# A new table of turns for a cross-attention kernel in f32: every operation numbered anew, with the arithmetic left as it was

## The chip, the cores and the metric

The kernel runs on one core of one Trainium2 chip. The metric is the device time of one execution in microseconds (us); smaller is better. A kernel's time is the median of its runs.

## What is computed

The reference, cut to what matters (B = 2 sequences of S = 2048 tokens, H = 640, 8 heads of 80, a context of 124 text tokens and 4 adapter tokens of 384 numbers each, all f32):

```python
query = x @ Wq
hs = mha(query, enc @ Wk, enc @ Wv)            # text attention, 124 keys
ca_q1 = einsum('btc,th->bch', ca, Wq_ca)[:, linspace(0, 383, 2048).astype(int), :]
ca_hs1 = mha(ca_q1, x, x)                      # attention over all 2048 tokens, 384 distinct queries
ca_hs2 = mha(ca_hs1 @ Wq, ca @ Wk_ca, ca @ Wv_ca)   # 4 keys
out = (hs + ca_hs2) @ Wout + b_out + x
```

## The kernel before, in words

The work is cut into 8 blocks of 512 tokens, (b, sb), and 16 units of 256 tokens, each two tiles of 128. The names below are those of the tiles, as rows of the profile show them; a number behind a name is a block, a unit or a part.

**The first block's rows.** `first_loads` (line 667) loads x's first 512 rows on SyncE as four transfers into `xz`, and Wq on ScalarE's queue as chunks into `wq_sb`. `idle_work` (line 768) gives TensorE 14 products of zeros (`unread<-zeros`) to run while there is nothing else. `x_first` (line 828) transposes the first block on TensorE (`pt_x`): two of its five column chunks from `xz` itself, three from `first_rows`, which VectorE gathers by five small copies for each tile. The results are copied to `xt` by VectorE or ScalarE.

**Later blocks.** `x_load` (line 1347) fetches the rows on SyncE by 13 transfers into `xi`, eight of them of 1024 short pieces (32x32 rows of 32 numbers; the second of each pair is issued in line 1363). When all have landed, VectorE turns them by five stream transposes into `xt`. `load_wout` (line 1187) loads Wout on SyncE too: two transfers of 640 KB, eight small ones.

**Queries.** `queries` and `queries_fast` (lines 1400 and 1542) multiply `xt` by `wq_sb` (`pq`), the later ones by a scheme of Strassen's kind that needs sums of blocks, `x_sums` and `wq_sums`; the same is done for the output with `hs` and `wout_sums`.

**The adapter.** `yz_block` (line 1754) turns each block into `zop`, by products (`pyz`), moves and a two-input operation on VectorE (`zop<-zop,low_z,zb`). `adapter` (line 1869) has two stages. In the first, TensorE writes scores `s1` of 2048 columns into one set of four PSUM banks (the quad), and VectorE takes the largest of each (`mx<-s`, 2.3 us); 24 of them for each sequence. There is one quad, so the next `s1` has to wait for the `mx` of the one before. In the second stage ScalarE reads the quad instead (`ea<-s`, exponentials, 1.9 us) and TensorE contracts `ea` with the rows `y_sb` (`acc`).

**Text attention.** `text_scores` and `softmax` (lines 2140 and 2178): scores `sc`, a maximum `m` on VectorE, exponentials `p` on ScalarE, a reciprocal `r`, `p<-p,r` on GpSimd, VectorE or ScalarE, a transpose `eb` on VectorE; `eb` goes to HBM and comes back turned as `pT`.

**Outputs.** `text_out_fast` (line 2392): `ph` from `pT`, copies and sums in `hs`, products `po` with `wout_sb` and `wout_sums`, and VectorE adds them into `x_more` or `last_rows`, which hold the residual. GpSimd adds the adapter's rows by an indirect transfer (line 2351). `stored` and `stored_half` (lines 2508 and 2499) store the rows from SyncE's or ScalarE's queue; the last unit goes out in four halves.

**What sets the order.** Nothing above is issued in the order in which it is written. Each stage is a generator that yields operations (`Do`). `Desk.run` (line 351) takes, of all that wait, the one with the lowest number in the table `Desk.TURNS` (lines 85 to 291), and the number's remainder by 6 names the engine (PE, ACT, DVE, POOL, SP, or none). So the table sets the order of each engine's instructions and, where an operation may run on several engines, which one takes it: copies out of PSUM on VectorE or ScalarE, sums on VectorE or GpSimd, stores on SyncE or ScalarE. On the chip each engine runs its own list in order and waits for semaphores of the others. In the profile nearly all of it carries the line of a helper: 396, 405 and 410 for TensorE's products, products by columns and transposes, 427 for VectorE, ScalarE and GpSimd, 447 for transfers.

Of the kernel before, what the change touches and what calls it, by code (L numbers as in the profile page):

```python
# [65 lines left out]
class Desk:  # L66
# [19 lines left out]
        ".1": [995], ".2": [44, 59, 60, 84, 96, 108, 114, 120, 126, 132, 150, 174, 198, 210, 234, 978], ".3": [608],  # L86
        ".4": [5, 52, 76, 82, 94, 106, 352, 412, 442], ".4.1": [37, 67, 169, 241, 265], ".5": [468, 499, 534, 547,
        558, 584, 590], ".6": [11, 17, 144, 162, 204, 222, 258, 294, 300, 329], ".6.1": [140], ".6.2": [188],
        ".6.3": [218], ".6.4": [284], ".6.5": [157], ".6.6": [194], ".6.7": [229], ".6.8": [253], ".6.9": [278],
        ".6.10": [314], ".6.11": [319], ".7": [290, 510, 530, 1058], ".8": [23, 29, 35, 180, 246, 270, 306, 360,  # L90
        384, 396, 420, 426, 456, 486, 540, 576, 636, 726, 792, 803], ".8.1": [404], ".8.2": [416], ".8.3": [518],
        ".8.4": [703], ".8.5": [935, 1003, 1064, 1069, 1334], ".8.5.1": [1174], ".8.5.2": [1258], ".8.5.3": [1301],
        ".8.5.4": [1307, 1372, 1529, 1531, 1541, 1597], ".8.5.5": [1426], ".8.5.6": [1414], ".8.5.7": [1481],
        ".8.5.8": [1619, 1660, 1781, 1783, 1937, 1975], ".9": [368, 377, 450, 474, 485, 522, 564, 575, 618, 624,
        635, 672, 708, 762, 786], ".9.1": [464], ".9.2": [493], ".9.3": [553], ".9.4": [596], ".9.5": [643], ".9.6":
        [650], ".9.7": [685], ".9.8": [770], ".9.9": [812], ".9.10": [817], ".10": [605, 678, 716, 734, 828, 848,
        858, 919, 926, 936, 950, 972, 1088], ".11": [656, 744, 834, 912, 942, 960, 1025, 1031, 1039, 1052, 1084,
        1168, 1264, 1360, 1408, 1471], ".11.1": [782], ".11.2": [872], ".11.3": [956], ".11.4": [968], ".11.5":
        [1016], ".12": [1103, 1113, 1364], ".13": [760, 778, 1270], ".14": [724, 1176, 1214, 1308, 1328, 1416, 1441,
        1446, 1465, 1490, 1642, 1834, 1870, 1948, 2782, 4306, 5614, 6568], ".15": [694, 699, 984, 1032, 1242, 1272,  # L100
        1343], ".15.1": [1076], ".15.2": [1094], ".15.3": [1279], ".15.4": [1315], ".16": [1509], ".17": [335, 1104,
        1141, 1147, 1157, 1160, 1183, 1196, 1220, 1285, 1352], ".17.1": [1544, 1588, 1592, 1612, 1715, 1721, 2596,
        2830, 3832, 4780], ".18": [341, 1139], ".19": [809, 2663], ".20": [346, 358, 382, 394, 436, 448, 508, 616,
        664, 671, 752, 824, 842, 854, 866], ".21": [881, 1794, 1843, 1861, 1877, 1880, 1897, 1958, 1982, 2029,
        2078], ".21.1": [1886, 1912, 2084, 2116, 2219, 2225, 2362, 2734, 3028, 5020], ".22": [893, 2201], ".23":
        [2171, 3683], ".24": [887, 1128, 1200, 1320, 1344, 1392, 1458, 1482, 1644, 1704, 1740, 1836, 1926, 1950,
        2016, 2154, 2165], ".24.1": [1573], ".24.2": [1495], ".24.3": [1807], ".24.4": [1963], ".24.5": [2213, 2239,
# [2484 lines left out]
```

## Time and profile before

| | us |
|---|---|
| the three runs | 574.08, 573.70, 573.08; median 573.70 |
| the profiled execution | 573.39 |
| its span, first to last instruction | 571.3 |
| TensorE busy in the span | 563.5 (99%) |
| VectorE, ScalarE, GpSimd busy | 394.3, 287.0, 159.9 (69%, 50%, 28%) |
| TensorE's granted clock | 1.0 throughout |
| TensorE waited for another engine, all waits that the view lists | 3.5 |

The profiled execution took 573.39 us, 2.1 us more than its span, and lies 0.31 us below the median of the runs. Matmuls are pipelined and their ends are modelled, each about a quarter of a microsecond past the start of the next, so a wait of TensorE shows as idle time only in so far as it is longer than that. Starts are not modelled; a wait is best read from the start of the instruction that waited and the end of what it waited for.

### The profile page before, as it was taken

Reading aid. Unit: us, or ns where it says so; the run is one execution under the profiler, and the core shown is the slowest. Engines: PE = TensorE matmul, PEld = TensorE weight load, DVE = VectorE, ACT = ScalarE, POOL = GpSimd, SP = SyncE. Lnnn points to the kernel's source line nnn. Section 1 sums busy time; section 2 is a strip of 40 time slices with the busy share of each in tenths; the row PEclk is TensorE's granted clock in tenths of the full one; section 3 lists DMA queues with packets and bytes.
Section 4 is the critical chain, followed back from the end, with each engine's and each line's share of the span. In section 5 each row is a group of like instructions: output and inputs, shape, how many; then the busy total and the mean of one; then the engine's idle time right before and its main releaser. Section 6 shows DMA issues by size and latency. Waiting matters only on the chain.

```text
span 571.3 us, 18875 instructions
## 1 busy us (share of the span) xinstructions
PE 563.5 (99%) x8069; PEld 309.8 (54%) x8069; DVE 394.3 (69%) x659; ACT 287.0 (50%) x806; POOL 159.9 (28%) x213
## 2 busy tenths in 40 slices
PE   8999999999999999999999999999999999999997
PEld 8885335455555455466554554554555444455553
DVE  4366999999998577458999999998332213544443
ACT  2021355645566899899876654524554674100000
POOL 9102041114440731100004350531203053045152
PEclk9999999999999999999999999999999999999999
DMA  8998485965978877446746979987375587788887
GB/s 246 211 247 136 130 162 149 170 187 138 209 214 156 213 182 211 146 129 195 230 157 200 317 190 310 244 237 241 72 263 120 162 199 231 247 209 213 265 185 206
DMA packets 145691, 113.21 MB, mean 198 GB/s; under 512 B 82548, under 2 KB 116980, under 8 KB 145608
## 3 DMA queue, kind: packets, MB, share of 16 engines
q1 hardware_dynamic: 137144, 95.43, 59.8%
q0 software_dynamic: 5632, 10.69, 11.5%
q10 hardware_dynamic: 2832, 5.90, 3.0%
q8 instruction: 63, 1.03, 0.8%
q14 instruction: 20, 0.16, 0.1%
HBM read 71.60 MB, written 40.39 MB: 196 GB/s over the span
## 4 chain that ended last, share of the span: by engine, by line
PE 93%; ACT 3%; DVE 3%; DMA 1%; issue 0%; SPq 0%; ACTq 0%
PE po L405 27%; PE pq L405 24%; PE sc L396 8%; PE acc L396 7%; PE ph L396 7%; PE s L396 7%; PE pq L396 4%; PE pyz L396 2%; ACT ea L427 2%; PE pv L396 1%; DVE mx L427 1%; PE pk L396 1%; DMA xz<-in_x_dram 1%; ACT p L427 1%; PE pt_wq L410 1%; PE pw L396 0%
## 5 line engine op out<-in xcount | busy, mean ns | idle before, releaser
L427 ACT ACTIVATE p<-sc,m 128x124 f32<-128x124 f32 x256 | 90.4, 382 | 43.1 <-DVE m L427 38.1
L427 DVE TENSOR_REDUCE mx<-s 128x4 f32<-128x2048 f32 x48 | 108.9, 2270 | 1.9 <-PE s L396 1.9
L427 ACT ACTIVATE ea<-s 128x2048 f32<-128x2048 f32 x48 | 90.5, 1886 | 32.5 <-PE s L396 32.0
L405 PE MATMUL po<-wout_sums,hs 128*32 128x320 f32 x1024 | 78.4, 434 | 0.1
L405 PE MATMUL po<-wout_sb,hs 128*32 128x320 f32 x928 | 72.3, 433 | 0.0
L427 POOL TENSOR_TENSOR p<-p,r 128x992 f32<-128x992 f32 x17 | 31.4, 1849 | 130.9 <-DVE r L427 130.9
L405 PE MATMUL pq<-xt,wq_sb 128*32 128x256 f32 (+1 forms) x928 | 66.4, 418 | 0.0
L427 DVE TENSOR_TENSOR last_rows<-last_rows,po 128x320 f32<-128x320 f32 x60 | 28.1, 480 | 44.0 <-PE po L405 43.9
L427 ACT ACTIVATION_READ_ACCUMULATOR p<-sc,m 128x1 f32 x256 | 57.2, 224 | 0.0
L427 DVE TENSOR_TENSOR x_more<-x_more,po 128x320 f32<-128x320 f32 x68 | 32.3, 481 | 34.7 <-PE po L405 34.2
L405 PEld LDWEIGHTS po<-wout_sums,hs 128*32 128x32 f32 x1024 | 33.3, 110 | 32.7 <-issue 2.8
L427 DVE TENSOR_REDUCE m<-sc 128x4 f32<-128x496 f32 x64 | 40.7, 661 | 14.1 <-PE sc L396 14.0
L396 PE MATMUL acc<-ea,y_sb 128*32 128x384 f32 (+2 forms) x768 | 50.2, 382 | 0.2 <-ACT ea L427 0.2
L396 PE MATMUL ph<-pT,vpad 128*32 128x256 f32 x768 | 48.0, 381 | 0.1
L405 PEld LDWEIGHTS po<-wout_sb,hs 128*32 128x32 f32 x928 | 30.1, 110 | 28.3 <-issue 1.6
L2351 POOL DMA_INDIRECT x_more<-o,query x17 | 26.6, 1564 | 64.9 <-DVE x_more L427 30.7
L405 PEld LDWEIGHTS pq<-xt,wq_sb 128*32 128x32 f32 x928 | 27.7, 110 | 28.0 <-issue 13.4
L427 ACT COPY hs<-ph 128x512 f32<-128x512 f32 (+1 forms) x25 | 13.4, 552 | 57.7 <-PE ph L396 57.7
L427 DVE STREAM_TRANSPOSE eb<-p 128x1024 f32<-128x1024 f32 x32 | 39.4, 1230 | 1.2 <-POOL p L427 1.1
L396 PEld LDWEIGHTS sc<-kmain,q 64*128 64x128 f32 x512 | 31.8, 187 | 12.6 <-issue 5.8
L427 POOL TENSOR_TENSOR hs<-hs 128x256 f32<-128x256 f32 x31 | 28.9, 1021 | 34.2 <-ACT hs L427 26.0
L396 PE MATMUL sc<-kmain,q 64*128 64x124 f32 x512 | 38.0, 285 | 0.0
(219 smaller groups left out, 834.5 us busy)
## 6 DMA issues: line engine op xcount, KB each, us to landing
kept<-eb SPq DMA_DIRECT2D x32, 512.0 KB, 4.7
pT<-kept SPq DMA_DIRECT2D x16, 1024.0 KB, 7.8
landing<-away SPq DMA_DIRECT2D x15, 512.0 KB, 4.8
xi<-in_x_dram SPq DMA_DIRECT2D x56, 128.0 KB, 4.1
x_more<-in_x_dram SPq DMA_DIRECT2D x17, 320.0 KB, 4.8
last_rows<-in_x_dram SPq DMA_DIRECT2D x15, 320.0 KB, 6.3
y<-yt SPq DMA_DIRECT2D x16, 256.0 KB, 2.9
y_sb<-y SPq DMA_DIRECT2D x32, 128.0 KB, 3.9
```

The lines of the kernel that those rows point to most:

```text
L396: self.pin(self.nc.tensor.matmul(out, lhsT, rhs, **kw))
L405: self.pin(self.nc.tensor.matmul(out[j : j + 32], lhsT[:, j : j + 32], rhs, **kw))
L410: self.pin(self.nc.tensor.transpose(out, in_, ident))
L427: self.pin(getattr(engine, what)(*args, **kw))
L2351: desk.pin(nc.gpsimd.indirect_dma_start(out=t, out_offset=None, in_=o2_of[b], in_offset=bass.IndirectOffsetOnAxis(ap=query[:, st : st + 1] ...
```

## The change

The table of turns is replaced by another; no other line of the kernel differs. What it does, counted over the program: 3787 of TensorE's 4494 matmuls stand in the same order as before, nearly all of the others in the first 44 us and behind 306 us. Six sums move from GpSimd to VectorE, eight copies (net) from ScalarE to VectorE, and two stores from SyncE to ScalarE. The number of matmuls and their shapes are the same.

The table has 206 lines; of one of them, before and now:

```diff
-        ".1": [995], ".2": [44, 59, 60, 84, 96, 108, 114, 120, 126, 132, 150, 174, 198, 210, 234, 978], ".3": [608],
+        ".1": [875], ".2": [44, 59, 60, 78, 90, 102, 108, 114, 120, 138, 198, 204, 282, 354, 522, 858], ".3": [428],
```

The numbers tell a reader nothing, so here are the instructions at three places, before and now.

**The first microseconds.** ScalarE's first instructions before; the first DMA row stands for Wq's chunks 0 and 1, one behind the other, and the copies move transposed rows of the first block out of PSUM:

```order
L447 DMA wq_sb<-in_L_xattn_Wq_dram 128x640 x2
L427 ACT_TABLE_LOAD
L427 COPY xt_0_164<-pt_x_0_191 128x256
L447 DMA wq_sb<-in_L_xattn_Wq_dram 64x640 x2
L427 COPY xt_0_164<-pt_x_0_214 128x256
L447 DMA wq_sb<-in_L_xattn_Wq_dram 64x640 x2
L427 COPY xt_0_164<-pt_x_1_223 128x384
```

And now:

```order
L447 DMA wq_sb<-in_L_xattn_Wq_dram 128x640
L427 ACT_TABLE_LOAD
L427 COPY xt_0_164<-pt_x_0_184 128x256
L447 DMA wq_sb<-in_L_xattn_Wq_dram 128x640
L447 DMA wq_sb<-in_L_xattn_Wq_dram 64x640 x2
L427 COPY xt_0_164<-pt_x_1_199 128x384
L427 COPY xt_0_164<-pt_x_0_215 128x256
```

Wq's chunk 1 is issued behind the first copy instead of ahead of it. On GpSimd, at the end of its masks, before (`vpad` and `ca` are cleared, then `ca` is filled by small transfers):

```order
L541 AFFINE_SELECT band_c_148<-band_c_148 128x4
L427 MEMSET vpad_107 128x768
L427 MEMSET vpad_108 128x768
L427 MEMSET ca_152 128x384
L427 DMA ca_152<-in_ctx_dram 4x384 x16
```

And now:

```order
L541 AFFINE_SELECT band_c_148<-band_c_148 128x4
L427 MEMSET ca_152 128x384
L427 DMA ca_152<-in_ctx_dram 4x384 x16
L427 MEMSET vpad_107 128x768
L427 MEMSET vpad_108 128x768
```

The two clears of `vpad` stand behind `ca` and its 16 transfers now. On TensorE, 7 products of zeros instead of 8 stand ahead of the first transpose, and the eighth is done later among the first products.

**The third block's rows and the first maxima.** SyncE's queue before, from Wout's two large transfers on (`xi_2` is the block b = 0, sb = 2; `k_away` is a store of keys):

```order
L447 DMA wout_sb<-in_L_xattn_Wout_dram 64x4x640 x2
L447 DMA xi_2_521<-in_x_dram 32x32x32
L1363 DMA xi_2_521<-in_x_dram 32x32x32
L447 DMA xi_2_521<-in_x_dram 32x16x16 x2
L447 DMA xi_2_521<-in_x_dram 32x32x32
L1363 DMA xi_2_521<-in_x_dram 32x32x32
L447 DMA k_away<-k_parts 32x4x248
```

And now:

```order
L447 DMA xi_2_476<-in_x_dram 32x32x32
L1363 DMA xi_2_476<-in_x_dram 32x32x32
L447 DMA xi_2_476<-in_x_dram 32x16x16 x2
L447 DMA wout_sb<-in_L_xattn_Wout_dram 64x4x640
L447 DMA xi_2_476<-in_x_dram 32x32x32
L1363 DMA xi_2_476<-in_x_dram 32x32x32
L447 DMA wout_sb<-in_L_xattn_Wout_dram 64x4x640
L447 DMA k_away<-k_parts 32x4x248
```

Wout's two transfers of 640 KB stand between the block's pieces instead of ahead of them. VectorE, between the first two maxima of the adapter, before:

```order
L427 TENSOR_REDUCE mx_0_563<-s1_0_0_0_0_704 128x4
L427 STREAM_TRANSPOSE xt_0_2_703<-xi_0_2_521 128x512
L427 TENSOR_SCALAR blk_v_127<-pt_vca_734,side2_83 128x4x2x4 x2
L427 TENSOR_TENSOR blk_v_127<-pt_vca_734,eighth_87 128x4x8 x2
L427 TENSOR_TENSOR first_rests_532<-pq_0_2_168,first_rests_532 128x256
L427 SCALAR_TENSOR_TENSOR zop_0_0_666<-zop_0_0_666,low_z_134,zs_0_0_1_700 128x512
L427 TENSOR_REDUCE counted_162<-steps_597 128x16
L427 TENSOR_TENSOR counted_162<-counted_162,first_161 128x16
L427 CAST query_111<-counted_162 128x16
L427 STREAM_TRANSPOSE xt_0_2_703<-xi_0_2_521 128x512 x2
L427 TENSOR_REDUCE mx_0_563<-s1_0_0_0_1_768 128x4
```

And now:

```order
L427 TENSOR_REDUCE mx_0_663<-s1_0_0_0_0_704 128x4
L427 COPY vpad_0_107<-pv_0_1_577 124x4x64
L427 COPY vpad_0_107<-pv_0_1_577 124x2x16 x2
L427 SCALAR_TENSOR_TENSOR zop_0_0_667<-zop_0_0_667,low_z_134,zs_0_0_1_702 128x512
L427 TENSOR_SCALAR blk_v_127<-pt_vca_735,side2_83 128x4x2x4 x2
L427 TENSOR_TENSOR blk_v_127<-pt_vca_735,eighth_87 128x4x8 x2
L427 COPY vpad_1_108<-pv_1_1_727 124x4x64
L427 COPY vpad_1_108<-pv_1_1_727 124x2x16 x2
L427 STREAM_TRANSPOSE xt_0_2_700<-xi_0_2_476 128x512 x3
L427 COPY vpad_1_108<-pv_1_0_719 124x4x64
L427 COPY vpad_1_108<-pv_1_0_719 124x2x16 x2
L427 TENSOR_REDUCE mx_0_663<-s1_0_0_0_1_767 128x4
```

Nine copies into `vpad` have come to VectorE from ScalarE, the counting is done earlier, and the three transposes of the third block's rows stand together ahead of the second maximum.

**A maximum of the second sequence.** VectorE near 303 us of the trace, before (the names end in numbers of their own in each program):

```order
L427 TENSOR_REDUCE m_1_7_1_4053<-sc_1_7_1_4035 128x4
L427 SCALAR_TENSOR_TENSOR zop_1_1_3403<-zop_1_1_3403,low_z_134,zb_1_1_1_4014 128x512
L427 STREAM_TRANSPOSE eb_11_0_4107<-p_0_830 128x1024
L427 TENSOR_TENSOR q_7_3752<-q_7_3752,pq_7_3_3983 128x2x256
L427 TENSOR_REDUCE mx_1_3167<-s1_1_1_0_0_4115 128x4
L427 TENSOR_TENSOR x_sums_873<-pq_7_4_4017,x_sums_873 128x256
L427 TENSOR_TENSOR wout_sums_4129<-wout_sb_100 128x640
L427 TENSOR_TENSOR wq_sums_834<-pq_7_4_4017,wq_sums_834 128x256
L427 RECIPROCAL r_1_7_4054<-r_1_7_4054 128x8
L427 TENSOR_REDUCE mx_1_3167<-s1_1_1_0_1_4158 128x4
```

And now:

```order
L427 TENSOR_REDUCE m_1_7_1_4046<-sc_1_7_1_4028 128x4
L427 TENSOR_TENSOR q_7_3752<-q_7_3752,pq_7_3_3977 128x2x256
L427 STREAM_TRANSPOSE eb_11_0_4106<-p_0_830 128x1024
L427 SCALAR_TENSOR_TENSOR zop_1_1_3400<-zop_1_1_3400,low_z_134,zb_1_1_1_4006 128x512
L427 TENSOR_REDUCE mx_1_3071<-s1_1_1_0_0_4112 128x4
L427 TENSOR_TENSOR wout_sums_4129<-wout_sb_100 128x640
L427 TENSOR_TENSOR x_sums_871<-pq_7_4_4011,x_sums_871 128x256
L427 RECIPROCAL r_1_7_4047<-r_1_7_4047 128x8
L427 TENSOR_TENSOR wq_sums_834<-pq_7_4_4011,wq_sums_834 128x256
L427 TENSOR_REDUCE mx_1_3071<-s1_1_1_0_1_4156 128x4
```

`zop` goes behind `q` and `eb`, the last ahead of the maximum; GpSimd's list here is the same (`p<-p,r`, then `wout_sums<-wout_sb`).

**The last stores.** TensorE's last products are the same four groups for unit 15 as before. Before, SyncE issued the last half of unit 15 and behind it a store of a whole tile of unit 8 (`last_rows`); now ScalarE issues that tile of unit 8 (`x_more`) behind the third half, and SyncE's last instruction is the last half (`last_rows`).

410 rows, old and new, of the table TURNS are left out of this document.

## The prediction, made before the changed kernel was run

> **What bounds the kernel now.** I read the page first, its busy times, its slices and the chain:
>
> ```profile
> PE 563.5 (99%) x8069; PEld 309.8 (54%) x8069; DVE 394.3 (69%) x659; ACT 287.0 (50%) x806; POOL 159.9 (28%) x213
> ...
> DVE  4366999999998577458999999998332213544443
> ...
> PE 93%; ACT 3%; DVE 3%; DMA 1%; issue 0%; SPq 0%; ACTq 0%
> ```
>
> TensorE (PE) is busy for 563.5 us of 571.3 and carries 93% of the chain. VectorE (DVE), at 69% over the whole, is full in slices 5 to 12 and 20 to 27 of 14.3 us. So I asked for the windows of these stretches, and for TensorE's waits (the last row is one of them):
>
> ```profile
> core 0: us, PE busy (x) PEld busy (x) DVE busy (x) ACT busy (x) POOL busy (x), PEclk, DMA share, GB/s
> 0.00:57.00 57.00, 55.43 (x412) 44.24 (x413) 28.90 (x106) 10.13 (x21) 19.03 (x92) 1.00 0.92 210
> 57.00:171.00 114.00, 114.00 (x1562) 55.62 (x1565) 111.97 (x146) 60.53 (x228) 32.15 (x24) 1.00 0.71 170
> 171.00:271.00 100.00, 99.63 (x1631) 56.03 (x1625) 67.14 (x112) 87.87 (x228) 19.80 (x24) 1.00 0.68 176
> 271.00:385.00 114.00, 112.39 (x1657) 59.74 (x1655) 110.23 (x136) 68.93 (x268) 35.21 (x31) 1.00 0.79 236
> 385.00:571.30 186.30, 182.03 (x2824) 94.16 (x2822) 76.08 (x164) 59.50 (x63) 53.68 (x43) 1.00 0.74 201
> ...
> PE s L396 <- ACT ea L427: 0.6, 3, 0.2
> ```
>
> TensorE's idle time is 1.57 us in the first window, 0, 0.37 and 1.61 in the next three, and 4.27 in the last, nearly all of that behind its last product. The work of TensorE is not changed, so what a new order can gain is small: these waits, those too short to show, and the tail. What it can lose has no such bound, above all in the two stretches where VectorE has 2.0 and 3.8 us to spare in 114.
>
> **The change, part by part.** I take TensorE's list first. Its products are the same, but it changes between shapes of the array 263 times instead of 261. From 57 to 171 us it makes dozens of such changes with 0.00 us idle, so one costs less than the quarter of a microsecond by which ends are modelled; between 0 and 0.25 each I take 0.12: **+0.25**.
>
> *The start.*
>
> ```profile
> 1.13 3.59 PE L396 MATMUL unread<-zeros 128*128 128x128 f32 x16 [1.13 <-DVE zeros L427]
> 4.90 0.41 PE L410 MATMUL pt_x<-ident,xz 128*128 128x128 f32 x2 [0.18 <-POOL band_z L541]
> ...
> 7.90 0.52 PE L410 MATMUL pt_x<-ident,first_rows 128*128 128x128 f32 x3 [0.26 <-DVE first_rows L427]
> ...
> 9.80 1.89 PE L396 MATMUL pq<-xt,wq_sb 128*128 128x256 f32 x8
> 6.21 1.78 DVE L427 COPY first_rows<-xz 128x64 f32<-128x64 f32 x5 [0.75 <-DMA xz<-in_x_dram]
> 8.37 0.62 DVE L427 COPY first_rows<-xz 128x64 f32<-128x64 f32 x5
> 5.80 1.41 POOL L427 MEMSET vpad<- 128x768 f32 x2
> 5.35 1.17 ACTq L447 DMA_DIRECT2D wq_sb<-in_L_xattn_Wq_dram  x2
> DMA to landing us min/median/max: 3.2/4.0/4.9
> ```
>
> Five copies of first rows last 1.78 us beside GpSimd's (POOL's) clears of `vpad` and `ca`, and 0.62 without them; the transposes at 7.90 wait for them. The 0.26 of that row stands behind the modelled end of a pair of passes, about 0.4 long, of which 0.22 is issue (as at 4.90): 0.43 lost. With the clears of `vpad` moved behind the transfers of `ca` it goes. What is late next is x's second tile, which landed before 6.21 and lands no later now, since Wq's chunk 1 (320 KB) no longer stands beside it. A filler that stood under the first wait now stands among products: two passes of 0.11, +0.22. Against it the first transposes (4.90) may come up to 0.3 earlier with x's rows; I take 0.2. Chunk 1 is issued behind the first copy, as the row at 5.35 is now, and takes 3.2 to 4.9 us (the last row, of `wq_sb`'s transfers from 5 to 12 us), so it lands between 8.5 and 10.2; its first product stood at 9.80 and would stand at 9.4. The wait is 0 to 0.8, nearer 0.1 by the median of 4.0. Sum of the start: −0.43 + 0.22 − 0.2 + 0.1 = **−0.3** (−0.6 to +0.4).
>
> A rule speaks against it. The first 16 passes start 0.22 apart and later ones 0.11, at a granted clock that reads 1.0 throughout. The Trainium skill, "TensorE: Matmul & The Clock Gate", Part 1, says that the array runs at half speed until a window of about 3.4 us has been busy, and that the window runs free. By it, 14 passes that end at 4.3 could miss the window; that is rival D below.
>
> *The first maxima.*
>
> ```profile
> 40.88 4.85 SPq L447 DMA_DIRECT2D xi<-in_x_dram  x3
> 58.24 0.70 DVE L427 STREAM_TRANSPOSE xt<-xi 128x512 f32<-128x512 f32 x1
> 63.37 2.25 DVE L427 TENSOR_REDUCE mx<-s 128x4 f32<-128x2048 f32 x1
> 65.93 0.51 PE L396 MATMUL s<-zop,cop 32*128 32x512 f32 x4
> DMA to landing us min/median/max: 7.8/7.8/7.8
> ```
>
> The second maximum ends at 65.62, 0.31 ahead of the `s` that needs its quad. Between the two maxima VectorE now has nine `vpad` copies (0.2 us each in steps), `zop` and four `blk_v` (1.3), and three transposes (0.65 each in steps): about 5.2 us behind the maximum that ended near 58.3, so the next starts near 63.6 and ends at 65.9, and TensorE, whose list is 0.2 longer by there, waits 0 to 0.3: **+0.1**. Behind this stands SyncE: Wout's two transfers, 7.8 us from issue to landing (the last row), now lie between the block's pieces, in a queue that held a piece for 4.85 us. The pieces had landed when VectorE came at 58.24; it comes at about 61 now, so a delay of up to 2.8 us is covered. More is rival C.
>
> *The maximum at 307 us.*
>
> ```profile
> 303.53 2.00 DVE L427 SCALAR_TENSOR_TENSOR zop<-zop,low_z,zb 128x512 fp32r<-128x512 f32 x1
> 305.46 1.23 DVE L427 STREAM_TRANSPOSE eb<-p 128x1024 f32<-128x1024 f32 x1
> 306.62 0.64 DVE L427 TENSOR_TENSOR q<-q,pq 128x512 f32<-128x512 f32 x1
> 307.19 2.27 DVE L427 TENSOR_REDUCE mx<-s 128x4 f32<-128x2048 f32 x1
> 310.89 2.23 DVE L427 TENSOR_REDUCE mx<-s 128x4 f32<-128x2048 f32 x1
> 303.44 1.55 POOL L427 TENSOR_TENSOR wout_sums<-wout_sb 128x640 f32<-128x640 f32 x1 [0.64 <-PE pq L405]
> 305.84 0.51 PE L396 MATMUL s<-zop,cop 32*128 32x512 f32 x4
> 309.52 0.51 PE L396 MATMUL s<-zop,cop 32*128 32x512 f32 x4 [0.44 <-DVE mx L427]
> 313.17 0.51 PE L396 MATMUL s<-zop,cop 32*128 32x512 f32 x4 [0.67 <-DVE mx L427]
> L427 DVE SCALAR_TENSOR_TENSOR zop<-zop,low_z,zb 128x512 fp32r<-128x512 f32 x1 | 0.7, 741 | 0.0
> ```
>
> `zop` takes 2.00 us while GpSimd sums from 303.44 to 304.99, and 0.74 elsewhere (the last row, from 290 to 303). Now `q` and `eb` come first, 0.64 and 1.23, and `zop` starts at about 305.4, behind GpSimd. The maximum then starts when its `s` is done, at 306.35, instead of 307.19. The wait at 309.52 goes (−0.44). The next maximum has the same 1.43 us of other work ahead of it, starts at 310.05 and ends at 312.3, where `s` comes at 313.17 − 0.67 − 0.44 = 312.06: the second wait shrinks to 0.24 (−0.43). I take **−0.8**. This rests on `x_sums<-pq` and `wq_sums<-pq` not being held by GpSimd's next two sums, which now start 1.2 us earlier, beside them:
>
> ```profile
> 209.97 0.68 DVE L427 TENSOR_TENSOR q<-q,pq 128x512 f32<-128x512 f32 x1
> 209.60 1.85 POOL L427 TENSOR_TENSOR p<-p,r 128x992 f32<-128x992 f32 x1 [1.65 <-DVE r L427]
> ```
>
> A sum with one input in PSUM runs at its usual 0.68 beside GpSimd. The Trainium skill, "GPSIMD Engine Reference", section 8, puts the contention on VectorE's instructions with two SBUF inputs (or in a two-port mode), and the trace agrees. Were every two-input sum held, the two would lose up to 1.5 us, and this term would be +0.3 instead.
>
> *Elsewhere.* From 57 to 271 us TensorE's list is the same but for small swaps, and so are the waits for `ea`. VectorE takes six more sums of 0.4 to 1.2 us, where GpSimd had them, but gives `p<-p,r` and two `x_sums` of the full stretch behind 271 to other places; its work in both full stretches stays within 0.3 us. From 306 to 566 us the outputs are in another order. The waits there were short (the last window shows no more than 0.2 us of idle ahead of the tail). I take **0** for them, with −1.2 (all the short ones go) and +2 (one as long as that at 313.17 in each 90 us) as ends.
>
> *The end.*
>
> ```profile
> 566.11 1.97 SPq L447 DMA_DIRECT2D out_dram<-x_more  x2
> 567.21 0.34 ACTq L447 DMA_DIRECT2D out_dram<-x_more  x1
> 568.17 0.41 SPq L447 DMA_DIRECT2D out_dram<-last_rows  x1
> ```
>
> The whole-tile store is the last and stands behind the last half in SyncE's queue, though its rows were ready. On ScalarE it goes out at 567.21 + 0.34 = 567.55, 0.6 earlier. Then the last half, issued as before near 567.75, is late next; it carries half the bytes. I take **−0.4** (−0.6 to 0).
>
> The sum: +0.25 − 0.3 + 0.1 − 0.8 + 0 − 0.4 = −1.15, so 572.2 against the profiled 573.39. That execution is 0.31 below the median of 573.70; from the median it is 572.5. I say **572.5**.
>
> **The rivals.** *A, the waits only move* (within 0.2%): the two waits at 309 and 313 are of one order among thousands, and a new order of the outputs brings its own. For it: VectorE's margins before the second maximum and before several adds are under 0.3 us. The price is that of one or two waits such as those (0.44 and 0.67): the gain of 1.15 shrinks to 0 or 0.5, 573.4.
>
> *B, more goes than I count*: the short waits of the outputs and of the `ea` stretch (0.6) fall away as well. −1.15 − 1.2 − 0.6 gives −2.95, 570.7. Against it: ScalarE's list in the `ea` stretch is the same.
>
> *C, slower, by SyncE's queue between 39 and 65 us.* Wout's 1.28 MB lie ahead of the last pieces of `xi_2`; the three transposes wait for them, and the second maximum stands behind the transposes. It decides from 2.8 us of delay on; past that, each us of delay is one of TensorE's, and from 4.0 on the kernel is slower than before. At the full 7.8 us of Wout's landing that is 5.0 us lost: 572.5 + 5.0 = 577.5; at 5 us, 574.7. For it: the DMA share is 0.92 up to 57 us, and the eight small pieces of Wout stand behind it as well. Against it: 1.28 MB at that window's 210 GB/s would be 6.1 us, but the pieces of `xi_2` no longer wait for Wout at their start, and SyncE was held by their number (4.85 us for three), which is the same.
>
> *D, TensorE's slow passes last longer* (also slower): if the pace does not rise at 4.3 us, the some 26 passes up to 8.3 us cost 0.11 more each, 2.9 less the 0.4 of waiting there: 572.5 + 2.5 = 575.0. For it: before, the pace rose during the last passes of the row at 1.13. Against it: the pause is 0.3 us of 3.4.
>
> *E, slower by new waits in the outputs* at their upper end, +2: 574.5.
>
> **How the numbers follow.** 0.2%, 1.15 us, is about what a measurement of this kernel can tell from no change, and my forecast stands just past it. The forecast has a chance of 0.42, half of it faster by more than 0.2% and half within; A 0.12, within; B 0.16, faster; C 0.13, D 0.05 and E 0.12, slower. That makes 0.37 faster, 0.33 within, 0.30 slower. The range reaches down to B (570.7) and up to between E and the far end of C, 576.5; below and above lie some 0.2.
>
> **What would show it.** In the profile of the changed kernel: the five copies near 6 us in 0.6; a first product of chunk 1 without a wait; `mx` in the chain near 64 us only if C holds, with `xi` as releaser of VectorE; `zop` at 0.74 and a maximum directly behind its `s` near 306; the last instruction a half store. The prediction is wrong if waits for `mx` or for adds sum to over 2 us, or if `pt_x` or `pq` waits for transfers in the first 15 us.

## The result, and the profile after

The changed kernel takes **579.94 us** (median; 581.00, 579.68, 577.76, 580.21) against 573.39 for the kernel before, timed beside it (572.89 to 574.08): a ratio of 1.0108, 95% interval 1.0088 to 1.0127. It is 6.5 us slower. I had said 572.5, with 576.5 as the upper end.

The profiled execution took 581.00 us, its span 579.3. The page's busy times, the granted clock in 40 slices (14.5 us each), and the chain:

```profile
PE 567.2 (98%) x8069; PEld 308.7 (53%) x8069; DVE 399.8 (69%) x673; ACT 284.2 (49%) x798; POOL 156.7 (27%) x207
...
PEclk9999999999999999999999998999999999999999
...
PE 85%; DVE 7%; ACT 5%; issue 1%; POOL 1%; DMA 1%; DVEq 0%; ACTq 0%; POOLq 0%
```

The chain has 85% of TensorE where it had 93, and 7% of VectorE where it had 3: TensorE now waits for others. Slice 25 (347.6 to 362.0 us) has a clock of 8. The same windows as before, in the same columns:

```profile
0.00:57.00 57.00, 55.06 (x404) 45.14 (x404) 26.18 (x101) 10.18 (x22) 19.18 (x92) 1.00 0.90 203
...
171.00:271.00 100.00, 99.16 (x1614) 56.07 (x1615) 69.13 (x116) 83.09 (x213) 18.55 (x23) 1.00 0.65 173
271.00:385.00 114.00, 109.11 (x1585) 57.75 (x1579) 106.09 (x133) 67.02 (x253) 34.18 (x25) 0.99 0.75 227
385.00:579.30 194.30, 189.84 (x2948) 94.63 (x2944) 86.26 (x178) 62.27 (x82) 55.57 (x45) 1.00 0.76 204
```

TensorE's idle time in these four is 1.94, 0.84, 4.89 and 4.46 us; it was 1.57, 0.37, 1.61 and 4.27. The window from 271 us on is the place to look. TensorE's own waits (sum, count, longest):

```profile
PE s L396 <- DVE mx L427: 2.7, 2, 2.1
...
PE pq L405 <- ACT q L427: 0.9, 1, 0.9
```

Idle time alone does not show passes at half pace, nor waits shorter than the modelled end of a matmul. So I also took, for each row of TensorE's list, its start less the time that all passes ahead of it need at the pace of unbroken rows of their shape, and looked at where this lag grows. That is a working from many rows, not a view:

| stretch (us of the changed kernel) | lag gained before | after | difference |
|---|---|---|---|
| 0 to 26, the start | 2.52 | 4.69 | **+2.17** |
| 26 to 222 | 4.09 | 3.99 | −0.10 |
| 222 to 230 | 0.21 | 1.28 | **+1.07** |
| 230 to 286 | 2.31 | 2.30 | −0.01 |
| 286 to 302 | 0.24 | 1.87 | **+1.63** |
| 302 to 308 | 0.68 | 0.48 | −0.20 |
| 308 to 324, the place of `zop` | 1.74 | 1.45 | −0.29 |
| 324 to 338 | 0.03 | 0.07 | +0.04 |
| 338 to 358 | 0.52 | 4.13 | **+3.61** |
| 358 to the last product | 4.35 | 4.08 | −0.27 |
| two changes of the array's shape more, as I had costed them | | | +0.25 |
| tail behind TensorE's last start | 4.60 | 4.63 | +0.03 |

The sum is +7.9, the difference of the spans (571.3 and 579.3). Four places make 8.5 of it.

**338 to 358.** VectorE, GpSimd and TensorE there:

```profile
343.92 1.69 POOL L2351 DMA_INDIRECT x_more<-o,query  x1 [0.17 <-DMA kept<-eb]
344.46 3.32 DVE L427 TENSOR_TENSOR hs<-hs 128x256 f32<-128x256 f32 x1
345.01 2.48 POOL L427 TENSOR_TENSOR p<-p,r 128x992 f32<-128x992 f32 x1
347.22 1.26 PE L405 MATMUL po<-wout_sb,hs 128*32 128x320 f32 x16
348.29 2.28 DVE L427 TENSOR_REDUCE mx<-s 128x4 f32<-128x2048 f32 x1
350.62 0.60 PE L396 MATMUL s<-zop,cop 32*128 32x512 f32 x4 [2.13 <-DVE mx L427]
351.15 2.36 PE L405 MATMUL po<-wout_sb,hs 128*32 128x320 f32 x16
```

A sum of `hs` that takes 0.42 us elsewhere takes 3.32 beside GpSimd's share `p<-p,r`, and ends 0.3 behind it. The maximum behind it is late by as much, and TensorE waits 2.13 us for it. Then 16 passes of `po` take 2.36 us, where the row at 347.22 took 1.26: half pace, and the 8 of slice 25. This sum is one of those that the change moved from GpSimd to VectorE. The six of which the description of the change speaks are a net number: by the two tables 23 operations of GpSimd's, sums and shares, are VectorE's now, and 17 went the other way.

The half pace belongs to this execution. The profiles of three kernels below that leave the sum where it is (eight products of zeros, the reciprocal, the store) show the wait of 2.13 us too, and full pace behind it. Against the kernel with the sum behind the maximum, TensorE loses 3.7 us at this place here and 2.6 in those three.

**286 to 302.** The same in small:

```profile
286.52 0.19 DVE L427 RECIPROCAL r<-r 128x8 f32<-128x8 f32 x1
286.63 2.27 DVE L427 TENSOR_TENSOR prod<-prod 128x288 f32<-128x288 f32 x2
286.79 1.95 POOL L427 TENSOR_TENSOR p<-p,r 128x992 f32<-128x992 f32 x1 [6.13 <-DVE r L427]
290.48 1.07 ACT L427 COPY q<-pq 128x512 f32<-128x512 f32 x2
291.60 1.93 PE L405 MATMUL pq<-x_sums,wq_sums 128*32 128x256 f32 x32 [0.92 <-ACT q L427]
```

The change put the reciprocal `r` ahead of the sums of `prod` and gave the share `p<-p,r`, which ScalarE had here, to GpSimd. The share starts as the sums do, and the groups of the two kernels (of before, then of after) show what that costs the smaller sums:

```profile
L427 DVE TENSOR_TENSOR prod<-prod 128x144 f32<-128x144 f32 x2 | 0.6, 308 | 0.1
```

```profile
L427 DVE TENSOR_TENSOR prod<-prod 128x144 f32<-128x144 f32 x2 | 2.1, 1070 | 0.1
```

Two sums, 0.6 us before and 2.1 now: one of them took about 1.8. The larger sum, which began 0.16 us ahead of the share, took 0.40; the smaller, which began 0.28 behind the share's start, was held. ScalarE's next exponentials wait for what VectorE makes of the sums, its copies of `q` (290.48) stand behind them, and TensorE waits 0.92 us for those.

**222 to 230.** SyncE and VectorE, some 10 us earlier (`eb` has one buffer, which is free when its store `kept<-eb` has landed):

```profile
206.03 1.25 DVE L427 STREAM_TRANSPOSE eb<-p 128x1024 f32<-128x1024 f32 x1
206.73 1.83 SPq L1363 DMA_DIRECT2D xi<-in_x_dram  x1
...
211.57 0.55 SPq L447 DMA_DIRECT2D kept<-eb  x1
217.04 1.25 DVE L427 STREAM_TRANSPOSE eb<-p 128x1024 f32<-128x1024 f32 x1 [4.39 <-DMA kept<-eb]
```

The transpose is done at 207.28, but its store goes out at 211.57, behind five other transfers, and the next transpose waits 4.39 us; a `q` of VectorE and TensorE's `sc` at 224.09 are late for it.

**The start.** Rows of TensorE and of ScalarE's queue:

```profile
5.21 0.66 PE L410 MATMUL pt_x<-ident,xz 128*128 128x128 f32 x2 [0.73 <-POOL band_c L541]
6.73 1.91 PE L396 MATMUL pq<-xt,wq_sb 128*128 128x128 f32 x8
9.11 3.87 ACTq L447 DMA_DIRECT2D wq_sb<-in_L_xattn_Wq_dram  x7
10.41 1.06 PE L396 MATMUL pq<-xt,wq_sb 128*128 128x128 f32 x8
19.31 1.89 PE L396 MATMUL pq<-xt,wq 128*128 128x256 f32 x8
```

Eight passes of `pq` take 1.91 us at 6.73 and 1.06 at 10.41: half pace up to about 9.6, where the kernel before had full pace from 4.9 on. The last row is a yardstick for the start: it is TensorE's first product with Wq's fifth part, behind the same products in both kernels but for one of zeros. It started at 17.37 before, the later the slower the start.

### The profile page after: what moved, and what is told of

Read it like the earlier page. It is cut to its first block, busy times and chain, and to the rows that moved or that the text cites. A ratio compares the mean times of both kernels' runs of the same rounds, so it can differ in the third digit from the quotient of the medians.

```text
span 579.3 us, 18853 instructions
## 1 busy us (share of the span) xinstructions
PE 567.2 (98%) x8069; PEld 308.7 (53%) x8069; DVE 399.8 (69%) x673; ACT 284.2 (49%) x798; POOL 156.7 (27%) x207
## 4 chain that ended last, share of the span: by engine, by line
PE 85%; DVE 7%; ACT 5%; issue 1%; POOL 1%; DMA 1%; DVEq 0%; ACTq 0%; POOLq 0%
PE po L405 26%; PE pq L405 22%; PE s L396 6%; PE ph L396 6%; PE acc L396 6%; PE sc L396 6%; PE pq L396 4%; DVE mx L427 3%; ACT ea L427 2%; PE pyz L396 2%; ACT p L427 1%; PE pv L396 1%; PE pk L396 1%; DMA kept<-eb 1%; DVE hs L427 1%
## 5 line engine op out<-in xcount | busy, mean ns | idle before, releaser
L427 POOL TENSOR_TENSOR p<-p,r 128x992 f32<-128x992 f32 x17 | 32.6, 1915 | 163.8 <-DVE r L427 130.9
L405 PEld LDWEIGHTS po<-wout_sums,hs 128*32 128x32 f32 x1024 | 31.7, 110 | 33.9 <-issue 3.4
L427 POOL TENSOR_TENSOR hs<-hs 128x256 f32<-128x256 f32 x25 | 24.2, 1042 | 50.6 <-ACT hs L427 22.4
L405 PE MATMUL pq<-xt,wq 128*32 128x512 f32 x280 | 34.1, 596 | 0.2 <-ACT p L427 0.2
```

The lines of the kernel that those rows point to most:

```text
L405: self.pin(self.nc.tensor.matmul(out[j : j + 32], lhsT[:, j : j + 32], rhs, **kw))
L427: self.pin(getattr(engine, what)(*args, **kw))
```

## The experiments

Each kernel moves a few operations in the table. For that, two lines of the class `Desk` ask a second, small table first; an entry gives an operation (its task and number) another turn and an engine:

```diff
-        turn = lambda op: self.TURNS[op.task.path][op.num]
+        turn = lambda op: self.MOVED.get((op.task.path, op.num), (self.TURNS[op.task.path][op.num],))
...
-            engine = self.ENGINES[turn(op) % len(self.ENGINES)]
+            engine = turn(op)[1] if len(turn(op)) > 1 else self.ENGINES[turn(op)[0] % len(self.ENGINES)]
```

My theory: a sum of VectorE with both inputs in SBUF waits for a sum of GpSimd that runs beside it; the change makes two such meetings ahead of a maximum or a copy that TensorE needs. The rivals: the places are slow for another reason (GpSimd's descriptors, the start's delay carried along), or the waits only move when one is taken away.

### The sum of hs at 344 us

The sum goes behind the maximum, still on VectorE:

```diff
+    MOVED = {('.60.3.6', 0): (9093, 'DVE')}
```

> The new order with one change on VectorE: the sum hs<-hs that took 3.32 us at 344.46 goes behind the maximum that followed it. Theory (the shared port): the sum, with two SBUF inputs, stood held while GpSimd's p<-p,r ran, and with it the maximum and the s product that waits for the quad (2.13 us shown, 2.2 by the starts), after which TensorE's passes were at half pace for 3.2 us (1.6 more). Moved, the sum costs no one: the wait near 350 goes, so do the slow passes behind it, and the time falls by 3.3 to 3.8, to some 576.3. Rival (VectorE is simply full here, the sum only showed it): the maximum comes at most 0.4 us earlier than by the sum's usual 0.42, the wait shrinks by less than half and the time stays above 578.

Measured: 576.18 us (575.75 to 576.52), ratio 1.0045 [1.0028, 1.0062]: 3.8 less than the changed kernel. In its profile the lag gained from 338 to 358 is 0.61 instead of 4.13. The stretched sum was the cost. But a sum that stands elsewhere cannot say what stretched it. So the sum keeps its place, and GpSimd's share moves instead, ahead of the indirect transfer:

```diff
+    MOVED = {('.69.2.2', 7): (9056, 'POOL')}
```

> The changed kernel with one edit at 344 us: GpSimd's share p<-p,r stands ahead of its indirect transfer instead of behind it, so that it can start at about 343.9 instead of 345.0 and end at about 345.8 to 346.4 instead of 347.5. VectorE's sum of hs keeps its old place (about 344.5) and so does the indirect's issue, now later. Theory (VectorE's sum is held until GpSimd's share ends, by the port they share): hs takes 1.3 to 1.9 us instead of 3.32, the maximum starts 1.4 to 2 us earlier, TensorE waits for it 0.1 to 0.7 instead of 2.13 us and keeps its clock, and the kernel takes 576.0 to 577.0 us, as with the sum behind the maximum. Rival 1 (GpSimd's writing of the indirect's descriptors holds hs): hs keeps 2.5 us or more, since that writing is only moved behind, and the time stays at 578.5 to 580. Rival 2 (hs is slow in this place for a reason of its own, not GpSimd's): 3.3 us, 579 to 580.

Measured: 577.49 us (576.66 to 578.00), ratio 1.0064 [1.0048, 1.0079]. The rows of the place:

```profile
343.06 1.84 POOL L427 TENSOR_TENSOR p<-p,r 128x992 f32<-128x992 f32 x1
343.80 1.38 DVE L427 TENSOR_TENSOR hs<-hs 128x256 f32<-128x256 f32 x1
345.06 1.69 POOL L2351 DMA_INDIRECT x_more<-o,query  x1 [0.17 <-issue]
345.69 2.28 DVE L427 TENSOR_REDUCE mx<-s 128x4 f32<-128x2048 f32 x1
348.02 0.51 PE L396 MATMUL s<-zop,cop 32*128 32x512 f32 x4 [0.19 <-DVE mx L427]
```

The sum starts 0.74 behind the share's start and takes 1.38 instead of 3.32, inside the 1.3 to 1.9 of the theory; it ends 0.28 behind the share's end, as in the changed kernel (347.78 and 347.49). TensorE waits 0.19. Rival 2 falls, and so does rival 1 as it was put: with the indirect behind the share, the sum does not keep 2.5 us. One thing stays open. In the changed kernel the sum's row begins 0.55 us ahead of the share's (344.46 and 345.01) and needs 0.42, so the share's row alone does not say why the sum was not done before it. Only the indirect's row (343.92 to 345.61) lies over that time. Beside an indirect alone, sums of `hs` took 0.38 to 0.43 in 86 places of the traces, so an indirect does not hold them as a rule; what held this one until the share began is not shown, since this kernel moved both. The time is 0.5 above the range, while the lag gained in the place is 1.33 instead of 4.13; the rest lies in the start and at 222, which differ from execution to execution (below).

Then the sum back on GpSimd, where the kernel before had it. (There it ran at 332.47, 8 us ahead of this share; here it stands directly ahead of it.)

```diff
+    MOVED = {('.60.3.6', 0): (9068, 'POOL')}
```

> The changed kernel with one part of the change undone: the sum of hs near 344 us on GpSimd again, where the kernel before had it, between the indirect transfer and the share p<-p,r; VectorE's list lacks it there. Theory (of the whole change it is this sum's move to VectorE, into the time of GpSimd's share, that costs 3.3 to 3.8 us): the maximum starts near 345.2 instead of 348.3, TensorE's wait of 2.13 us goes with the half pace behind it, and the kernel takes 576.0 to 577.0 us, as with the sum behind the maximum. Rival (GpSimd is what is late here: with one sum more, 1.0 us, its share ends 1 us later, and the transpose of eb and the next indirect with it): a new wait of TensorE of 0.5 to 1 us behind 348, 577 to 578.

Measured: 577.30 us (576.70 to 578.01), ratio 1.0068 [1.0051, 1.0085]. The maximum, the sums behind it and TensorE:

```profile
343.13 2.28 DVE L427 TENSOR_REDUCE mx<-s 128x4 f32<-128x2048 f32 x1
343.80 2.46 POOL L427 TENSOR_TENSOR p<-p,r 128x992 f32<-128x992 f32 x1
345.33 1.56 DVE L427 TENSOR_TENSOR hs<-hs 128x256 f32<-128x256 f32 x2
350.67 0.51 PE L396 MATMUL s<-zop,cop 32*128 32x512 f32 x4 [0.30 <-DVE mx L427]
```

The lag of the place is 0.83, so the wait and the half pace went. The rival is right in part: GpSimd's share now meets another sum of `hs` (the two of the row take 1.56 instead of about 0.8), and 0.30 of a wait is left at 350.67. The maximum itself, whose input lies in PSUM, ran its usual 2.28 beside the share.

### The reciprocal at 286 us

`r` goes behind the sums of `prod`, so that GpSimd's share starts behind them:

```diff
+    MOVED = {('.65.2.2', 6): (7527, 'DVE')}
```

> The new order with one change on VectorE: the reciprocal r at 286.52, which releases GpSimd's p<-p,r, goes behind the two prod sums and their three followers. Theory (the shared port): the second prod took 1.83 us because p<-p,r ran beside it; then ScalarE's q copies came 1.4 us late and TensorE waited 0.92 (1.1 by the starts). Moved, the two prod sums last 0.8 together, q is in time, the wait at 291.6 goes and 1.0 to 1.4 us with it, 578.7. Rival: the wait is for ScalarE's own list (eight p<-p,r of 2.54 us stand ahead of the copies there), and then it stays at 0.5 us or more. p<-p,r itself comes 2.9 us later; if its transpose eb at 293.32 becomes late, 0.3 us come back there.

Measured: 578.12 us (577.22 to 578.63), ratio 1.0084 [1.0067, 1.0100], 1.8 less than the changed kernel. The time alone does not settle it: this interval overlaps that of the changed kernel (1.0088 to 1.0127), and the kernel with an eighth product of zeros (below), which touches nothing here, came out 1.3 lower too. In the profile:

```profile
285.12 0.79 DVE L427 TENSOR_TENSOR prod<-prod 128x288 f32<-128x288 f32 x2
...
286.95 1.84 POOL L427 TENSOR_TENSOR p<-p,r 128x992 f32<-128x992 f32 x1 [7.70 <-DVE r L427]
```

The sums take 0.79 again, and the lag of 286 to 302 falls from 1.87 to 0.37. GpSimd still has the share; what cost was the time at which it ran.

### The store of eb at 211 us

```diff
+    MOVED = {('.61.2.1', 9): (5331, 'SP'), ('.46.1', 3): (5332, 'SP')}
```

> The new order with one change in SyncE's queue: the store kept<-eb, issued at 211.57 though its eb was done at 207.3, goes ahead of four others, and y<-yt behind it. Theory (SyncE's queue and the one eb buffer): the next eb waited 4.39 us on VectorE for that store to land (216.95), and the sums, the reciprocal and q behind it came late, so that TensorE lost 1.05 near 224. Issued near 208.6, the store lands near 213, VectorE waits under 1 us, q is done before TensorE asks for it, and 1.0 us goes, 578.9. Rival: q's lateness comes from GpSimd's p<-p,r (1.85 us, waited for at 222.2), which hangs on the r at 220.03 and so on TensorE's own sc; then the wait at 224 stays at 0.6 or more.

Measured: 578.53 us (577.76 to 579.62), ratio 1.0094 [1.0077, 1.0111], 1.4 less than the changed kernel, again with overlapping intervals, and the lag at 222 is 0.21. That alone would look settled. But profiles of other kernels that keep the late store show 0.20 (the one with eight products of zeros), 0.21 (the sum on GpSimd), 0.57 (the sum behind the maximum), about 1.3 (the reciprocal) and 1.31 (the share ahead). In the two with 0.2 the store landed 3.6 and 3.8 us after its issue and `eb` waited 2.1 us; in the other three and the changed kernel it landed after 5.0 to 5.6, and `eb` waited 3.7 to 4.4. The time in SyncE's queue, from the end of `eb` to the issue, differed less (3.7 to 4.3). With the store ahead the lag was 0.21 in all five profiles that have it so. So the late place makes the wait possible, the time to landing decides whether TensorE feels it, and the price is 0 to 1.1. Why the landing differs is not shown.

### The start

An eighth product of zeros ahead of the first transposition, in the changed kernel:

```diff
+    MOVED = {('.2', 9): (123, 'PE')}
```

> The new order with one change: the eighth product of zeros stands ahead of the first transpose again, instead of behind it. Theory (the clock): in the new order TensorE was idle from 4.28 to 5.21 us and its passes then kept starting 0.21 us apart until 9.6, 2.1 us lost; with eight products the pause begins at 4.7 and is half as long, and the passes from 5.2 on start 0.11 apart, so the first products of chunk 1 (12.18 in the new order) come near 10 us and the time is about 2.1 below the new order's 579.9, 577.8. Rival 1 (a free-running window): the pace rises at a moment of its own, whatever stands ahead; then this run's profile may be slow or fast, its runs scatter by some 2 us as those of the new order do (577.8 to 581.0), and their median stays near 579.9. Rival 2 (x's rows, which landed at 5.1 instead of 4.8, are what costs): the pause stays and the passes are slow as before.

Measured: 578.62 us (578.24 to 580.04), ratio 1.0096 [1.0077, 1.0114]. The yardstick starts at 18.48 instead of 19.31, but by the same yardstick other kernels with the changed start unaltered stand at 18.96, 17.92, 18.01, 18.62 and 18.06 (the sum behind the maximum, the reciprocal, the store, the share ahead, the sum on GpSimd). So one profile does not tell it. From the other side, in the kernel before, seven products of zeros instead of eight, and then Wq's chunk 1 late:

```diff
+    MOVED = {('.2', 9): (151, 'PE')}
```

> The kernel before, with one edit: seven products of zeros instead of eight ahead of the first transposition of x, the eighth behind it, as the change has it. Theory (the pause of TensorE ahead of the first transposition sets how long its passes run at half pace): the pause grows by one product of zeros, 0.3 to 0.4 us, the passes reach full pace later and the time rises by 0.5 to 1.5 us, to 574.0 to 575.0. Rival (the start of the changed kernel is late because Wq's second chunk is issued late): no change, 573.3 to 573.8.

```diff
+    MOVED = {('.4.1', 1): (165, 'ACT')}
```

> The kernel before, with one edit: ScalarE issues Wq's second chunk behind its first eviction of x's columns instead of second of all, as the change has it. Theory (late chunk): every later chunk of Wq lands later, TensorE waits for wq_sb between 9 and 18 us, and the time rises by 0.5 to 1.5 us, to 574.0 to 575.0. Rival (only the pause ahead of the first transposition counts): within 0.3 us of the kernel before, 573.2 to 573.8.

Measured, beside a kernel before of 573.19: 573.44 (ratio 0.9998 [0.9989, 1.0008]) and 573.99 (1.0007 [0.9998, 1.0016]). The missing product shows no cost. In that profile, though, x's rows came early and the pause stayed at 0.17 us, so the theory of the pause was hardly put to the test. With the late chunk the time is −0.1 to 0.9 us above the kernel before, and the yardstick stands at 17.87, 0.5 behind. But no product waits for `wq_sb` in that profile; its passes start 0.21 apart from 4.79 to about 6.8 us. So its 0.5 is half pace, and the theory of the late chunk is not borne out by it.

### Several mends together

```diff
+    MOVED = {('.60.3.6', 0): (9093, 'DVE'), ('.65.2.2', 6): (7527, 'DVE'), ('.61.2.1', 9): (5331, 'SP'), ('.46.1', 3): (5332, 'SP'), ('.64.3.9', 2): (13645, 'SP')}
```

> The changed kernel with four moves: hs's sum behind the maximum (as tried alone, about -3.8 us), the reciprocal behind the sums of prod (about -1.5), the store of eb ahead (0 to -1, since the wait differed from run to run), and, new, unit 8's last tile stored by SyncE ahead of the last half instead of by ScalarE behind it. If the costs add up: 580 - 3.8 - 1.5 - 0.5 - 0.4 = 573.8, between 573.2 and 574.5, and the tail behind TensorE's last start shrinks from 4.6 to 4.2 us. Rival (each mend moves the meeting of DVE's and GpSimd's sums to another place): 575 or more, with stretched sums in new places. Rival for the end (the last half lands last anyhow): tail 4.6.

Measured: **574.21 us**, ratio 1.0008 [0.9999, 1.0017]. The costs add up: 5.7 of the 6.5 us are gone with the three mends and the move at the end. What the end's move did is told below. In its profile one new wait shows: an `eb` at 381.56 waited 0.68 us for the store of the one ahead of it, and TensorE 0.50 at 383.63. The next kernel's profile does not have it, and no stretched sum stands ahead of a wait of TensorE's. With two points of the start of before as well:

```diff
+    MOVED = {('.2', 9): (123, 'PE'), ('.4.1', 1): (64, 'ACT'), ('.60.3.6', 0): (9093, 'DVE'), ('.65.2.2', 6): (7527, 'DVE'), ('.61.2.1', 9): (5331, 'SP'), ('.46.1', 3): (5332, 'SP'), ('.64.3.9', 2): (13645, 'SP')}
```

> The kernel of the run ahead of this one (three mends and the end), with the start of the kernel before in two points: eight products of zeros ahead of the first transposition, and Wq's second chunk issued second of all by ScalarE. Theory (the start's extra 1 to 2 us come from these two): 1 to 2 us less than that run, 571.8 to 573.0, so at or below the kernel before; TensorE's loss of the first 20 us falls from 3.3 to 4.7 us to about 2.5. Rival (the loss there varies with the clock's own window, whatever the start's order): equal to that run within 0.4 us, with a loss of 3 us or more.

Measured: 573.80 us, ratio 1.0005 [0.9996, 1.0014]: 0.4 less, within what the two spread. The rival is nearer: the yardstick is 18.49 here and 18.26 without the two. What both profiles share is in ScalarE's and SyncE's queues; the rows of this run:

```profile
7.78 4.92 ACTq L447 DMA_DIRECT2D wq_sb<-in_L_xattn_Wq_dram  x7
10.09 0.77 SPq L447 DMA_DIRECT2D xi<-in_x_dram  x1
...
16.68 1.97 PE L396 MATMUL pq<-xt,wq_sb 128*128 128x256 f32 x8 [0.56 <-issue]
```

Wq's last seven transfers take ScalarE 4.92 us while SyncE already issues the next block's pieces, and TensorE's products with the last chunk start late. Before, SyncE began at 11.95, when they were out. So the whole start of before, 49 operations of the first 12 us of the plan, on top of the three mends and the end (a few of the entries):

```diff
+    MOVED = {('.4.1', 1): (67, 'ACT'), ('.6.6', 0): (194, 'DVE'), ('.4.1', 2): (169, 'ACT'), ('.4.1', 3): (241, 'ACT'), ('.4.1', 4): (265, 'ACT'), ('.20', 1): (358, 'SP'),
...
```

> The changed kernel with the three mends and the end's move of the earlier run (574.2 us), and the whole start of the kernel before: every instruction of the first 12 us of the plan in the place and on the engine that it had there, SyncE's transfers of xi behind Wq's last chunk too. Theory (what the mends left is the start: its loss of 3.6 to 3.9 us against 2.5, now with Wq's last chunk issued from about 8.6 in 2.5 us instead of from 7.7 in 5): the loss of the first 20 us falls to 2.4 to 2.7 us and the time to 572.2 to 573.0, at or just below the kernel before. Rival (the start's loss varies by the clock's window whatever the order): loss 3 us or more, 573.5 to 574.5.

Measured: 573.97 us, ratio 1.0004 [0.9995, 1.0013], though the start is as forecast: lag 2.55, yardstick 17.40. The gain was taken at 72 us:

```profile
63.20 0.36 SPq L447 DMA_DIRECT2D k_parts<-k_away  x1
70.56 1.02 ACT L427 CAST krest<-k_parts 128x992 fp32r<-128x992 f32 x1 [2.26 <-DMA k_parts<-k_away]
```

TensorE came there 1.1 us earlier, SyncE did not, and the keys' rests had not come back: 1.2 us lost. Here a mend did uncover the next wait. The last kernel sends the keys away and fetches them earlier in SyncE's queue, and turns two adds round:

```diff
+    MOVED = {('.11', 13): (1266, 'SP'), ('.11', 14): (1273, 'SP'), ('.65.3.11', 3): (12277, 'DVE'),
...
```

> The earlier run with the start of before (574.0 us; its profile: TensorE's loss of the first 20 us 2.55 as forecast, but a new one of 1.2 us at 72, where ACT's krest waits 2.26 us for the transfer k_parts<-k_away), with three moves more: SyncE stores the last k_away ahead of the eight transfers of wout_sb and fetches k_parts right behind them; VectorE adds x_more ahead of last_rows at 494. Theory (the krest wait took back what the start gave, 1.1 of 1.2 us; the add 0.3): 574.0 - 1.2 - 0.3 = 572.5, between 572.0 and 573.2, below the kernel before. Rival (the fetch lands late because SyncE's transfers share the 16 engines, not because of its place in the queue): the wait at 72 stays over 0.5 us, 573.3 to 574.2.

Measured: **572.37 us** (571.63 to 573.38) against 573.09, ratio 0.9988 [0.9979, 0.9997]. The same rows of SyncE and ScalarE:

```profile
62.05 0.37 SPq L447 DMA_DIRECT2D k_parts<-k_away  x1
68.58 1.02 ACT L427 CAST krest<-k_parts 128x992 fp32r<-128x992 f32 x1
```

The transfer is issued 1.15 us earlier and `krest` no longer waits, so its place in the queue was what counted. What the two adds gave was not tried alone. This version beats the changed kernel by far, and the one before by 0.7 us (0.1%) by an interval that ends just below 1.

## Why the prediction was wrong

The sum was −1.15; the spans say +7.9. Point by point:

**"Elsewhere ... I take 0."** This is the step that failed: +5.9 there. I counted the six sums that come to VectorE by their own length and looked at VectorE's margin in each stretch. I did not lay them beside GpSimd's list, although I had the price in hand: `zop` at 2.00 instead of 0.74 beside one of GpSimd's sums. I used that rule at the one place where the change takes a meeting away (307 us), and never asked where it makes a new one. The six were a net number besides, and a net number hides the places: 23 operations went to VectorE and 17 came back. The change makes two meetings ahead of something that TensorE needs: `hs` at 344 (3.61, about 1 of it by the half pace of that execution; moving the sum, moving the share and undoing the part each take 2.8 to 3.5 away) and `prod` at 286 (1.63, of which the reciprocal's move takes 1.5). The store of `eb` (1.07 in the profile, 0 to 1.1 by execution) is the third; the bound of +2 for waits of the outputs did not think of SyncE. Rival E had the kind, new waits in the outputs, but at most 2 us of them, and one place alone cost more. The sign that I had named, waits for `mx` of over 2 us, came: 2.7.

The Trainium skill, "GPSIMD Engine Reference", section 8, says that GpSimd shares its SBUF interfaces with VectorE, with contention for VectorE's instructions that have two SBUF inputs. The traces agree: `hs` and `prod` were held, the maximum with its input in PSUM was not (2.28 beside the share, with the sum on GpSimd). I had quoted the rule in the prediction and drawn from it only what it spared.

**Rival D, "TensorE's slow passes last longer", chance 0.05.** It came about in the profile: half pace up to 9.6 us, 2.2 lost in the start where I had −0.3. I held the pause of 0.3 us against a window of 3.4; the row at 5.21 shows 0.73, and the first transposes, which I had 0.2 earlier, came 0.31 later. The cause of the −0.43 did go: five copies of `first_rows` take 0.64, and no transpose waits for them. The Trainium skill, "TensorE: Matmul & The Clock Gate", Part 1, adds that the window runs free, so that the same kernel shows another number of slow passes in each run. The traces agree: seven profiles with the changed start unaltered have the yardstick at 17.92 to 19.31, mean 18.45; with the start of before it stood at 17.37, 17.40 and, in the last kernel, 17.79. So the start costs about 1 us on average. Part of that is no matter of the clock. In three of the seven profiles TensorE stands idle for 0.4 to 0.6 us ahead of the products with Wq's last chunk, whose transfers share the time with SyncE's pieces. And my +0.1 for chunk 1 (0 to 0.8) was too narrow: its first products waited 0.72 and 1.21 us for `wq_sb` in two of the seven (the sum behind the maximum, the share ahead), and not at all in the others, that of the changed kernel among them. How much of the 1 us is pace and how much is Wq stays open, since no kernel held the window still.

**The maximum at 307: −0.8, measured −0.3.** The mechanism held. The rows:

```profile
308.12 0.68 DVE L427 TENSOR_TENSOR q<-q,pq 128x512 f32<-128x512 f32 x1
309.90 0.75 DVE L427 SCALAR_TENSOR_TENSOR zop<-zop,low_z,zb 128x512 fp32r<-128x512 f32 x1
310.95 2.29 DVE L427 TENSOR_REDUCE mx<-s 128x4 f32<-128x2048 f32 x1 [0.30 <-PE s L396]
314.34 0.37 ACT L427 CAST wq_sums<-pq 128x256 fp32r<-128x256 f32 x1 [0.61 <-DVE x_sums L427]
314.75 0.42 DVE L427 TENSOR_TENSOR wq_sums<-pq,wq_sums 128x256 fp32r<-128x256 f32 x1 [0.33 <-ACT wq_sums L427]
315.32 1.12 PE L396 MATMUL sc<-kmain,q 64*128 64x124 f32 x15 [0.25 <-DVE wq_sums L427]
317.42 0.51 PE L396 MATMUL s<-zop,cop 32*128 32x512 f32 x4 [0.55 <-DVE mx L427]
```

`zop` takes 0.75, `q` is not held, the maximum waits for its `s` instead of the reverse, and the first wait is gone. What the term rested on held too: `wq_sums`, with one input in PSUM, takes its usual 0.42 beside GpSimd's sum (314.05 to 315.60). The second part was mis-sized. I took the same 1.43 us of work between the two maxima; it took 1.85. The sums are the same, but `x_sums` stands behind `wout_sums` (0.82) now instead of ahead of it. ScalarE's `wq_sums` waits for `x_sums`, and VectorE waits 0.33 for ScalarE. So the second wait stayed at 0.55, with 0.25 for `sc` ahead of it.

**The first maxima: +0.1, measured −0.1 (26 to 222 us as a whole).** Right, and rival C did not come: `mx` at 65.11 starts without a wait, and the transposes of `xt` had their pieces.

**The end: −0.4, measured 0.** I had the whole-tile store (`x_more`) going out from ScalarE's queue ahead of SyncE's last half. It goes out behind it:

```profile
572.83 3.16 ACTq L447 DMA_DIRECT2D out_dram<-last_rows  x3
575.11 0.34 SPq L447 DMA_DIRECT2D out_dram<-last_rows  x1
576.09 0.41 ACTq L447 DMA_DIRECT2D out_dram<-x_more  x1
```

With the tile's store moved ahead on SyncE, the tail was 4.30, 4.38, 3.84 and 4.49 us in four kernels, and 4.60 to 4.63 in those with the changed end: 0.1 to 0.8 less. But an unaltered end of before gave 4.60 and 4.85, so a single tail tells little; 0.3 is likely.

## What to carry to other kernels

When an order is changed, lay VectorE's instructions with two SBUF inputs beside GpSimd's long ones over the whole list, not only where the old order had a meeting, and count a meeting in which GpSimd began first as the wait to the end of GpSimd's instruction plus all that stands behind it. Count the places, not the net number of moves. Judge a moved sum by what waits behind it: 3.3 us on VectorE cost TensorE 2.6 to 3.7 us since a maximum followed, while in the kernel before a sum of `hs` held to 1.66 us at 395.99 left TensorE without a wait. And read a place in several executions before giving it a price: the start and the store at 211 moved by 1 us with no edit near them.

## What the runs showed of the hardware that I had not expected

A held sum does not run at a slower rate. Sums of `hs` that a sum or share of GpSimd's held until it was done ended 0.28 to 0.29 us behind its end, whether they took 0.53, 0.85, 1.38 or 1.66 us; the smaller `prod` ended 0.16 behind it, `zop` 0.55. A sum that began first was not held, by as little as 0.16 us (`prod` at 286.63, 0.40; `zop` at 342.42, 0.74 beside a sum of GpSimd's from 342.64), and then GpSimd's row was the longer: 1.95 instead of 1.84 for that share. The sum at 344.46 is the exception, as told above. GpSimd's share also reads 2.46 to 2.48 us where its row starts about 0.6 us before the row ahead of it has ended, an indirect or, in the kernel with the sum on GpSimd, a sum; that is overlap in the rows, with VectorE held or not.

A pause of 2.13 us was followed by half pace in one execution (the rows at 350.62 above, a clock of 0.89 from 345 to 360 us) and not in three others with the same pause (clock 1.00, 16 passes of `po` in 1.28). The Trainium skill, "TensorE: Matmul & The Clock Gate", section "Why this matters for your kernels", allows gaps of up to about 3 us between bursts; by these rows 2.1 can be too much.
